# A gated feed-forward layer with quantized second product: seven-product form for the last eight slots of the first batch, weight sums moved into the second batch, down_w turned through memory

## The chip, the cores and the metric

The kernel runs on one core of one Trainium2 chip. A core has five engines with queues of their own: TensorE (PE, matmuls, with its weight loads shown as PEld), VectorE (DVE), ScalarE (ACT), GpSimd (POOL) and SyncE (SP), which here issues nearly all DMAs. Each engine works its queue in order; semaphores tie them together. The metric is device time in microseconds of one execution. The kernel before took 734.88 us, the median of three runs (734.56 to 737.32).

## The reference

`x` is 4 batches of 1024 tokens of 512 numbers, `cond` 4 x 128, `up_w` 4096 x 512, `down_w` 512 x 2048. Cut to what matters:

```
scale = cond @ norm_w.T + 1.0
h  = x * (scale[:, None, :] * rsqrt(mean(x * x) + EPS))
u  = h @ up_w.T
val, gate = split(u, 2)
h  = val * gelu(gate)                     # exact GELU
hq = round(h * 127 / max|h| per token) / scale
wq = sign-like rounding of down_w to -1, 0, 1 times its mean magnitude
y  = hq @ wq.T + x
```

All numbers are fp32. The kernel gets the precision of the first product by writing each operand as a high and a low fp16 part and adding three products of the four; the second product is exact in bf16 by fp8.

## The kernel before, in words

**Slots.** The 2048 values and 2048 gates are cut into 16 slots of 128 rows of each (`NJ` = 16). One slot of one batch is one unit of work: the product of a 128-row value block and a 128-row gate block with all 1024 tokens. Slots are numbered through the four batches: slot 16 is the first of the second batch. `H` keeps the results of 18 slots.

**Two ways to do a slot.** In the first batch, `first_batch(j)` calls `plain_half` twice. Each half is 512 tokens: `plain` does 12 matmuls for the gate (4 pieces of the 512 features, 3 high/low terms each) and 12 for the value, 48 in a slot. In the later batches `slot(g)` treats the block as a 2 x 2 block product and does it with seven products of half size in place of eight (`product`, 6 matmuls each, 42 in a slot). The price is sums: seven combinations of the token blocks (`Tokens.sums`, `XP` and `t_view`) and seven of the weight blocks (`s_sums`), again split into high and low parts.

In `slot`, TensorE does products 0, 4 and 1 of slot g, then product 3 of slot g-1, 5 of g, 2 of g-1, and 6 of g. They accumulate onto each other: ScalarE copies bank A to bank B before product 1, copies E into `v`, copies A into `t2` (that copy stands ahead of product 6, which writes the same bank), and applies the two GELUs; VectorE multiplies and adds. The hooks `early`, `x`, `y`, `z` and `mid` are places between these steps where the caller puts further work.

**Weights.** In the first batch each slot's weights are loaded (`w_load`), scaled by a power of two per row (`w_range`, `w_gain`, `w_scale`), split into high and low (`w_rows`, or TensorE's transposes for the first three slots) and turned by a transposing DMA into a tile of three that take turns (`s_tile`). The sums of the weights, needed from the second batch on, are also made in the first batch: `s_sums` on GpSimd (four 128x256 operations), `s_high` on ScalarE, `s_low` on GpSimd, and `s_spill` writes all seven to `s_dram`. Later batches fetch them with `s_load_x` and `s_load_y`; the sums of slots 3 to 15 lie there unturned and are turned on the way in.

**The rest of the first batch.** `d_load`, `d_sum`, `d_round` and `d_put` bring down_w, take its mean magnitude and round it to three values, after which a transposing DMA turns it straight into `wd`. `Tokens` prepares the second batch: norm on ScalarE and GpSimd, `scale`, `sums` on GpSimd, `high`, `low`, and a transposing DMA (`turn`). `pair_max` takes the largest magnitude of each token over slots.

**The later batches.** After a batch's last slot the largest value per token over all partitions is needed: `token_max` calls `partition_all_reduce` on GpSimd, once for each half of the tokens, in places x and z of the next batch's slot 0. `get_ready` does a dummy reduction of that kind beforehand. Then `token_scale` on VectorE, the rounding (`quant_scale`, `quant_round`, `quant_up`, `quant_down`) in slots 2 to 9 and the second product in slots 10 to 13 (`Pair`). The order of the instructions is the order in which the code is written; a small planner (`Filler`, with costs and due places) hands out the rounding work in batches 2 to 4.

Of the kernel before, what the change touches and what calls it, by code (L numbers as in the profile page):

```python
# [50 lines left out]
def glu_quant_kernel(  # L51
# [30 lines left out]
    DVE.memset(neghalf, -0.5)  # L82
    unmagic = cpool.tile([P, 1], F32, name="unmagic")
# [16 lines left out]
    s_dram = tc.dram_tile([NJ, P, 7 * 2 * HALF], F16, name="s_dram")  # L100

# [27 lines left out]
    XP = XP.rearrange("p (l k t) -> p l k t", l=2, k=NK)  # L129
    S_more = R[:, 0, 4096 : 4096 + 7 * HALF].bitcast(F16).rearrange(  # L130
        "p (c w f) -> p c w f", c=7, w=2
    )
    A21 = R[:, 0, 6144 : 6144 + 768].bitcast(F16).rearrange("p (n w f) -> p n w f", n=3, w=2)
# [12 lines left out]
    def pow2_floor(t):  # L146

        ti = t.bitcast(I32)
        DVE.tensor_scalar(ti, ti, EXPONENT, None, ALU.bitwise_and)
# [107 lines left out]
    iv = {}  # L257
# [4 lines left out]

    def wf(j):

        return H[:, 11 if j == 2 else 15 + j % 2].rearrange("p t (n f) -> p (t n) f", n=2)
# [16 lines left out]
    def w_factor(j, am, t0=0, t1=2):  # L282
        t = slice(t0, t1)
        pow2_floor(am)
        DVE.tensor_scalar(sw[:, j, t], am, 2.0**-100, 1.0 / W_UP, ALU.max, ALU.mult)
        if j not in iv:
            iv[j] = sm.tile([P, 2], F32, name=f"iv_{j}", tag="iv", bufs=3)
        DVE.reciprocal(iv[j][:, t], sw[:, j, t])
# [4 lines left out]
    def w_gain(j):  # L293
        DVE.tensor_scalar(sg0[:, j, :], sw[:, j, :], dx[:, 0:1], None, ALU.mult)
# [4 lines left out]
    LATE = 6  # L299

    def w_scale(j, ts=(1, 0), eng=None):
        eng = eng or (ACT if j >= ROWS else POOL)
        for t in ts:
            w, r = wn(j)[:, t], iv[j][:, t : t + 1]
            if eng is ACT:
                ACT.activation(w, w, AF.Copy, scale=r)
            else:
                eng.tensor_scalar(w, w, r, 1.0, ALU.mult, ALU.mult)
# [11 lines left out]
    def a_parts(j):  # L320

        s = s_tile(j)
        return s[:, 5:7], s[:, 3] if j >= ROWS else A21[:, j % 3], s[:, 4]

    def w_rows(j):
# [4 lines left out]
        ACT.copy(n[:, :, 0], f)  # L330
        DVE.tensor_tensor(n[:, :, 1], f, n[:, :, 0], ALU.subtract)
        SP.dma_start_transpose(
            s_tile(j)[:, 3:7].rearrange("p n w (k f) -> p (n w k) f", k=2), v
        )
# [19 lines left out]
    def w_evac(j):  # L354
        for n in range(2):
            ACT.copy(wf(j)[:, 2 * n : 2 * n + 2].rearrange("p n f -> p (n f)"), pw[j][n])

    def s_sums(j):
        if j >= ROWS:
            v = wn(j).rearrange("p t (n f) -> p t n f", n=2)  # L360
            a11, a12, a21, a22 = v[:, 1, 0], v[:, 1, 1], v[:, 0, 0], v[:, 0, 1]
        else:
            a11, a12, a21, a22 = (wf(j)[:, n] for n in range(4))
# [5 lines left out]
    def s_parts(j):  # L369
        s = s_tile(j)  # L370
        s4 = A21[:, j % 3 : j % 3 + 1] if j >= ROWS else s[:, 3:4]
        return (s[:, 0:3], sf[:, 0:3]), (s4, sf[:, 3:4])

    def s_high(j):
        for s, f in s_parts(j):
            ACT.copy(s[:, :, 0], f)

    def s_low(j, eng):
        for s, f in s_parts(j):
            eng.tensor_tensor(s[:, :, 1], f, s[:, :, 0], ALU.subtract)  # L380

    def s_spill(j):
        def out(c0, c1, v):
            SP.dma_start(
                out=s_dram[j, :, c0 * 2 * HALF : c1 * 2 * HALF],
                in_=v.rearrange("p c w f -> p (c w f)"),
            )

        s = s_tile(j)
        if j < ROWS:  # L390
            out(0, C_ALL, s)
            return
        out(0, 3, s[:, 0:3])
        out(4, C_ALL, s[:, 4:])
        out(3, 4, A21[:, j % 3 : j % 3 + 1])

    def s_load(g, c0, c1, turn=False):
        s, d = s_tile(g)[:, c0:c1], s_dram[g % NJ, :, c0 * 2 * HALF : c1 * 2 * HALF]
# [5 lines left out]
    def s_load_x(g):  # L404
        s_load(g, Y_TO, C_ALL)
        s_load(g, 0, Y_FROM, g % NJ >= ROWS)

    def s_load_y(g):
        if g % NJ < ROWS:
# [38 lines left out]
    def d_round(n):  # L448

        dn = d_part(n)  # L450
        ACT.activation(dn, dn, AF.Copy, scale=wsc, bias=MAGIC)
# [3 lines left out]
    def d_put(n):  # L455
# [5 lines left out]
        if y:  # L461
            SP.dma_start_transpose(wd[:, n // 4, u], tn[-1])
# [17 lines left out]
    class Tokens:  # L480
# [73 lines left out]
        def low(self, eng):  # L554
            for n, f in self.parts():
# [11 lines left out]
    def product(c, g, ps, start, stop):  # L567
# [3 lines left out]
        o = ps.rearrange("p (a t) -> p a t", t=P)  # L571
        for n, (w, l, k) in enumerate(TERMS):
            PE.matmul(  # L573
                o, s[:, w, k, :], tv[:, :, c, l, k, :],
# [24 lines left out]
    def gain(g, t):  # L599
        return sg[g // NJ][:, g % NJ, t : t + 1]  # L600
# [40 lines left out]
    def slot(  # L641
        g, x=nothing, y=nothing, z=nothing, early=nothing, mid=(nothing,) * 3, late=nothing
# [11 lines left out]
        if up:  # L654
# [4 lines left out]
            ACT.copy(pb, cur["A"])  # L659
            cur["E"] = bank("E", 2, name=f"E_{g}")  # L660
# [36 lines left out]
    def pair_max(b, i, h, pairs=1):  # L697

        v = h_slots(b * NJ + 2 * i, 2 * pairs)[:, :, h].rearrange("p j t -> p t j")
# [56 lines left out]
    def grid_of(b, i, h):  # L756
        return h_slots(b * NJ + 2 * i, 2)[:, :, h], q_view(b)[:, :, h, 2 * i : 2 * i + 2]
# [238 lines left out]
    def second_part():  # L996
# [11 lines left out]
    D_ROUND = {5: (0, 1), 6: (2,), 7: (3,), 9: (4,), 10: (5,), 11: (6,), 12: (7,)}  # L1008
    D_MEAN = 4
    TOKENS = {6: 0, 8: 1, 10: 2, 12: 3}  # L1010
    LARGEST = {
        4: (0, 0, 2), 5: (0, 1, 2), 8: (2, 0, 2), 10: (2, 1, 2), 12: (4, 0, 2), 13: (4, 1, 2),
# [548 lines left out]
```

## Time and profile before

| | |
|---|---|
| median of 3 runs | 734.88 us (734.56 to 737.32) |
| the profiled execution's own time | 733.24 us |
| its span on the core | 731.4 us |
| TensorE busy | 720.9 us, 99% |
| VectorE busy | 587.2 us, 80% |
| ScalarE busy | 396.1 us, 54% |
| GpSimd busy | 195.8 us, 27% |
| first batch, slots 0 to 15 | to 188.4 us |
| second batch begins | 188.4 us |

The profile is of one execution. A row of the timeline reads: start in us, duration, engine, line of the kernel, operation, written and read tiles, shape, how many in a row, and in square brackets how long the engine had stood idle and what ended that. "issue" names idle time in which the engine waited for nothing that the profile shows. Matmuls are pipelined, so their cost is read from the step between rows rather than from a row's duration. In the view of waits, the three numbers are the total in us, how often, and the longest.

### The profile page before, as it was taken

The numbers are of one execution on the slowest core, as the hardware profiler recorded it, in microseconds if no ns is written. First come the engines' busy times: TensorE is split into PE (matmuls) and PEld (weight loads), VectorE is DVE, ScalarE is ACT, GpSimd is POOL, SyncE is SP. The second block draws the span as 40 slices with busy tenths as digits, with TensorE's granted clock in tenths as the row PEclk, the third lists the DMA queues.
The fourth block names the chain that finished last, engine by engine and source line by source line (L and its number), as shares of the span: only waits on it lengthen the run. The fifth ranks groups of instructions, "written<-read, shape, count | busy, mean of one in ns | idle before, by whom it ended". The sixth has DMA issues, their size and how long they took to land.

```text
span 731.4 us, 10126 instructions
## 1 busy us (share of the span) xinstructions
PE 720.9 (99%) x3661; PEld 358.9 (49%) x3661; DVE 587.2 (80%) x805; ACT 396.1 (54%) x629; POOL 195.8 (27%) x207
## 2 busy tenths in 40 slices
PE   7999999999999999999999999999999999999998
PEld 3544444444444446655444445665444444445744
DVE  6977889887498899797689887787678888755897
ACT  5868875872236675444335676543433665332274
POOL 1379886666200032450010030461020000000100
PEclk9999999999999999999999999999999999999999
DMA  6759998987544554886735646756934545452253
GB/s 233 252 165 307 291 286 233 254 199 180 165 94 106 134 121 147 191 164 172 194 100 102 130 101 173 187 146 165 226 98 106 91 100 115 103 103 90 87 189 115
DMA packets 203982, 117.30 MB, mean 160 GB/s; under 512 B 165382, under 2 KB 174487, under 8 KB 203932
## 3 DMA queue, kind: packets, MB, share of 16 engines
q1 hardware_dynamic: 203642, 116.33, 62.3%
q8 instruction: 28, 0.46, 0.3%
q10 hardware_dynamic: 290, 0.33, 0.2%
q14 instruction: 22, 0.18, 0.1%
HBM read 54.22 MB, written 23.09 MB: 106 GB/s over the span
## 4 chain that ended last, share of the span: by engine, by line
PE 87%; DVE 4%; POOL 4%; DMA 2%; ACT 1%; issue 1%; SPq 0%; POOLq 0%; DVEq 0%; ACTq 0%
PE A L573 34%; PE E L573 17%; PE B L573 8%; PE po L844 8%; PE pg L588 6%; PE pv L588 6%; PE po_end L793 4%; DVE gm L707 1%; PE po L793 1%; DMA H<-in_x_dram 1%; POOL xt L529 1%; DMA SXY<-H 1%; POOL H L367 1%; PE po_B L844 0%; POOL R L380 0%
## 5 line engine op out<-in xcount | busy, mean ns | idle before, releaser
L573 PEld LDWEIGHTS <-SXY 128*128 128x128 f16 x2016 | 197.3, 98 | 232.3 <-issue 0.6
L573 PE MATMUL A<-R,SXY 128*128 128x512 f16 x1152 | 266.3, 379 | 0.0
L573 PE MATMUL E<-R,SXY 128*128 128x512 f16 x576 | 140.0, 379 | 0.1
L671 DVE SCALAR_TENSOR_TENSOR H<-A,sg,t 128x512 f32<-128x512 f32 x48 | 36.0, 750 | 73.3 <-PE A L573 73.1
L588 PEld LDWEIGHTS <-SXY 128*128 128x128 f16 x486 | 47.4, 98 | 59.0 <-issue 1.7
L765 DVE TENSOR_TENSOR H<-H,am 128x1024 f32<-128x1024 f32 x64 | 76.2, 1216 | 0.0
L723 POOL PARTITION_ALL_REDUCE am<-R x8 | 14.3, 1793 | 230.4 <-DVE R L709 230.4
L684 ACT ACTIVATE t<-t,sg 128x512 f32<-128x512 f32 x48 | 34.6, 721 | 70.3 <-DVE t L681 70.2
L707 DVE TENSOR_REDUCE gm<-H 128x512 f32<-128x1024 f32 (+1 forms) x50 | 71.6, 1433 | 0.8
L573 PE MATMUL B<-R,SXY 128*128 128x512 f16 x288 | 70.0, 379 | 0.0
L588 PE MATMUL pg<-R,SXY 128*128 128x512 f16 x252 | 57.8, 379 | 0.3 <-DMA SXY<-H 0.3
L844 PE MATMUL po<-wd,R 128*128 128x256 fp8e4 (+1 forms) x448 | 56.8, 275 | 0.0
L588 PE MATMUL pv<-R,SXY 128*128 128x512 f16 x234 | 54.4, 379 | 1.1 <-DVE H L616 1.0
L844 PEld LDWEIGHTS <-R 128*128 128x128 bf16 (+1 forms) x480 | 47.0, 98 | 12.8
L668 ACT ACTIVATE t<-B,sg 128x512 f32<-128x512 f32 x48 | 33.0, 687 | 36.5 <-PE B L573 36.5
L477 POOL TENSOR_SCALAR ssq<-ssq 128x2 f32<-128x2 f32 x12 | 3.6, 298 | 176.8 <-ACT xt L507 124.1
L651 ACT COPY t<-A 128x512 f32<-128x512 f32 x48 | 27.9, 582 | 39.5 <-PE A L573 39.2
L659 ACT COPY B<-A 128x512 f32<-128x512 f32 x48 | 27.4, 572 | 39.0 <-PE A L573 38.6
L773 ACT ACTIVATE H<-H 128x1024 f32<-128x1024 f32 x38 | 39.9, 1050 | 14.1 <-DVE H L765 14.1
L663 ACT COPY v<-E 128x512 f32<-128x512 f32 x48 | 28.1, 585 | 31.3 <-PE E L573 27.8
L690 DVE SCALAR_TENSOR_TENSOR H<-v,sg,t 128x512 f32<-128x512 f32 x48 | 36.6, 762 | 7.4 <-ACT t L684 7.4
L777 ACT ACTIVATE R<-H 128x1024 bf16<-128x1024 f32 x38 | 40.1, 1055 | 0.8
(205 smaller groups left out, 978.3 us busy)
## 6 DMA issues: line engine op xcount, KB each, us to landing
SXY<-s_dram SPq DMA_DIRECT2D x57, 256.0 KB, 3.0
s_dram<-SXY SPq DMA_DIRECT2D x18, 384.0 KB, 3.0
H<-in_L_cond_up_w_dram SPq DMA_DIRECT2D x13, 512.0 KB, 5.1
SXY<-s_dram SPq DMA_DIRECT2D x39, 128.0 KB, 3.1
xr<-in_x_dram SPq DMA_DIRECT2D x19, 256.0 KB, 3.3
out_dram<-xr SPq DMA_DIRECT2D x19, 256.0 KB, 2.6
H<-in_x_dram SPq DMA_DIRECT2D x8, 512.0 KB, 8.0
R<-in_L_cond_down_w_dram SPq DMA_DIRECT2D x8, 512.0 KB, 6.9
```

Of the source, the lines that this page charges most:

```text
L573: PE.matmul(o, s[:, w, k, :], tv[:, :, c, l, k, :], start=start and n == 0, stop=stop and n == len(TERMS) - 1, skip_group_check=True,)
L588: PE.matmul(ps, a[k // 2][:, w, k % 2, :], XP[:, l, k, h * TOK : (h + 1) * TOK], start=n == 0, stop=n == len(terms) - 1,)
L668: ACT.activation(cur["t1"], pb, AF.Gelu, scale=gain(g, 1))
L671: DVE.scalar_tensor_tensor(h_half(g - 1, 0), prev["A"], gain(g - 1, 0), prev["t1"], ALU.mult, ALU.mult)
L684: ACT.activation(prev["t2"], prev["t2"], AF.Gelu, scale=gain(g - 1, 1))
L690: DVE.scalar_tensor_tensor(h_half(g - 1, 1), prev["v"], gain(g - 1, 0), prev["t2"], ALU.mult, ALU.mult)
L707: DVE.tensor_reduce(gm[0], v, AX.X, ALU.max, apply_absolute_value=True)
L765: DVE.tensor_tensor(v, v, r.to_broadcast([P, 2, TOK]), ALU.mult)
L773: ACT.activation(v, v, AF.Copy, bias=MAGIC)
L777: ACT.activation(q, by_tile(v), AF.Copy, bias=-MAGIC)
L793: PE.matmul(po.rearrange("p (y c o) -> p y c o", c=2, o=P), q[:, a, h, j], wd8[:, :, j // n, j % n, :, y0:y1].rearrange("p c o y -> p y c o"),
L844: PE.matmul(po, w[:, j], m, start=start and j == 0, stop=stop and j == n - 1, skip_group_check=True,)
```

## The change

- **Slots 8 to 15 of the first batch** (`FAST` = 8) go through `slot` in seven-product form (`fast_slot`); slots 0 to 7 stay plain (`plain_slot`). The token sums of the first batch, which this needs, are made by the new class `First`: GpSimd adds parts of `XP`, and high and low parts go to `XT`, which lies in `wd` for that time.
- **The sums of the weights of slots 0 to 7** are not made in the first batch. `Held` loads these weights again during slots 14 to 21 (`HELD_FROM` = 14), scales them on GpSimd, adds (`sums_of`, GpSimd), casts (`high`, ScalarE), subtracts (`low`, GpSimd) and spills them unturned. `held_first` stands in `early`, `held_next` around `x`.
- **The second batch takes slot 8 first** (`of_slot`, `TURNED` = 8): 8 to 15, then 0 to 7. Slots 8 to 15 lie turned in `s_dram`; 0 to 7 are turned on the way in.
- **down_w** goes to a DRAM tile (`d_dram`) and is turned from there by `d_turn` in the second batch's slot 1. `d_round` moves from ScalarE to GpSimd.
- `pow2_floor`, `w_factor` and `w_gain` use two-tensor forms with constant tiles (`emask`, `undo_up`) in place of scalar forms. `pair_max` covers two slots each time. The places of many steps in the first batch change.

The diff, cut to its core:

```diff
+    def s_turn(j):
+        SP.dma_start_transpose(
+            s_tile(j)[:, 0:4].rearrange("p n w (k f) -> p (n w k) f", k=2), S_rows
+        )
+    class Held:
+        def __init__(self, j):
+            self.j = j
+            self.w = wpool.tile([P, 2, D], F32, name=f"hw_{j}", tag="xn", bufs=1)
+            SP.dma_start(out=self.w, in_=up_v[j])
+        def sums(self):
+            j = self.j
+            for t in range(2):
+                w = self.w[:, t]
+                POOL.tensor_scalar(w, w, iv[:, j, t : t + 1], 1.0, ALU.mult, ALU.mult)
+            self.f = wpool.tile([P, 4, HALF], F32, name=f"hf_{j}", tag="xt", bufs=1)
+            sums_of(self.w, self.f)
+        def high(self):
+            v = wpool.tile([P, C_ALL, 2, HALF], F16, name=f"hr_{self.j}", tag="nx", bufs=1)
+            self.r = v[:, 0:4]
+            ACT.copy(self.r[:, :, 0], self.f)
+        def low(self):
+            POOL.tensor_tensor(self.r[:, :, 1], self.f, self.r[:, :, 0], ALU.subtract)
+        def spill(self):
+            s_spill_rows(self.j, self.r.rearrange("p n w f -> p (n w f)"))
...
     def d_round(n):
         dn = d_part(n)
-        ACT.activation(dn, dn, AF.Copy, scale=wsc, bias=MAGIC)
+        POOL.tensor_scalar(dn, dn, wsc, MAGIC, ALU.mult, ALU.add)
...
         if y:
-            SP.dma_start_transpose(wd[:, n // 4, u], tn[-1])
+            SP.dma_start(out=d_dram[n // 2], in_=tn[-1])
+    def d_turn():
+        for n in range(1, ND, 2):
+            SP.dma_start_transpose(wd[:, n // 4, d_at(n)[1]], d_dram[n // 2])
...
-    D_ROUND = {5: (0, 1), 6: (2,), 7: (3,), 9: (4,), 10: (5,), 11: (6,), 12: (7,)}
+    D_ROUND = {4: (0, 1, 2, 3), 5: (4, 5, 6, 7)}
+    D_PUT = {4: (0, 1), 5: (2, 3), 6: (4, 5), 7: (6, 7)}
-    TOKENS = {6: 0, 8: 1, 10: 2, 12: 3}
+    TOKENS = {5: 0, 7: 1, 9: 2, 11: 3}
...
+    def held_first(g):
+        i = g - HELD_FROM
+        if 0 < i <= FAST:
+            held[i - 1].spill()
+        if 0 <= i < FAST:
+            held[i].sums()
+            if i + 1 < FAST:
+                held.append(Held(i + 1))
+    def held_next(g, then=nothing):
+        mine = 0 <= g - HELD_FROM < FAST
+        if mine:
+            held[g - HELD_FROM].high()
+        then()
+        if mine:
+            held[g - HELD_FROM].low()
...
+    def fast_slot(j, sc):
+        n = j + 2
+        t = toks.get(j)
+        odd = t is not None and j not in TOKENS
+        def early():
+            held_first(j)
+            next_tokens(j + 1)
+            if n < NJ:
+                s_sums(n)
+            if j + 5 < NJ:
+                w_load(j + 5)
+            w_next(j)
+            largest(j, 0, 1)
+        def second():
+            if t and not odd:
+                t.norm()
+            elif odd:
+                t.high()
+        def x():
+            if n < NJ:
+                s_high()
+                s_low()
+            held_next(j)
+            if j in turns:
+                turns.pop(j)()
+            if j + 1 < NJ:
+                s_spill(j + 1)
+            if t and not odd:
+                t.scale(sc)
+                t.sums()
+            elif odd:
+                t.low(0, 2, DVE)
+            else:
+                largest(j, 1, 3)
...
+            if b == 1 and j == 1:
+                d_turn()
...
-            slot(g, lambda: run("x"), lambda: run("y"), lambda: run("z"), early, mid, late)
+            x = lambda: held_next(g, lambda: run("x"))
+            slot(g, x, lambda: run("y"), lambda: run("z"), early, mid, late)
```

## The prediction

> **What bounds the kernel now.** I read the page first: busy times, clock and chain.
>
> ```profile
> span 731.4 us, 10126 instructions
> PE 720.9 (99%) x3661; PEld 358.9 (49%) x3661; DVE 587.2 (80%) x805; ACT 396.1 (54%) x629; POOL 195.8 (27%) x207
> ...
> PEclk9999999999999999999999999999999999999999
> ...
> PE 87%; DVE 4%; POOL 4%; DMA 2%; ACT 1%; issue 1%; SPq 0%; POOLq 0%; DVEq 0%; ACTq 0%
> ```
>
> TensorE is busy 99% at full clock and carries 87% of the chain. So matmuls taken away are worth their issue time, and work on another engine costs nothing until TensorE waits for it. The timeline of TensorE gives the price of a slot; here one plain slot, the two stalls late in the first batch, and a seven-product slot of the second:
>
> ```profile
> 103.35 2.75 PE L588 MATMUL pg<-R 128*128 128x512 f16 x12
> 105.94 2.75 PE L588 MATMUL pv<-R 128*128 128x512 f16 x12
> 108.53 2.75 PE L588 MATMUL pg<-R 128*128 128x512 f16 x12
> 111.12 2.75 PE L588 MATMUL pv<-R 128*128 128x512 f16 x12
> 113.71 2.75 PE L588 MATMUL pg<-R,SXY 128*128 128x512 f16 x12
> ...
> 164.39 2.75 PE L588 MATMUL pv<-R,SXY 128*128 128x512 f16 x12 [1.05 <-DVE H L616]
> 175.49 2.75 PE L588 MATMUL pv<-R 128*128 128x512 f16 x12 [0.58 <-DVE H L616]
> ...
> 210.45 1.46 PE L573 MATMUL E<-R,SXY 128*128 128x512 f16 x6
> 211.74 2.75 PE L573 MATMUL A<-R,SXY 128*128 128x512 f16 x12
> ```
>
> Twelve matmuls step 2.59 us, so one costs 0.216; a plain slot is 48 (10.36), a seven-product slot 42 (9.07).
>
> Then GpSimd, in its waits and its timeline around the end of the first batch, where the all-reduces over partitions (token_max) stand:
>
> ```profile
> POOL ready L716 <- issue: 19.0, 3, 6.7
> ...
> 176.24 0.67 POOL L380 TENSOR_TENSOR R<-H,R 128x256 f16<-128x256 f32 x1
> 182.99 0.38 POOL L716 PARTITION_ALL_REDUCE ready<-ready  x1 [6.08 <-issue]
> 191.57 1.81 POOL L723 PARTITION_ALL_REDUCE am<-R  x1 [8.20 <-DVE R L709]
> 197.82 1.78 POOL L723 PARTITION_ALL_REDUCE am<-R  x1 [4.44 <-DVE R L709]
> ```
>
> Before an all-reduce that follows ordinary arithmetic, GpSimd stands idle with nothing to wait for: 19.0 us over three times, 6.33 each. get_ready, a dummy all-reduce, takes that idle time early, when GpSimd has nothing else to do; the two real ones follow without it. The way back to arithmetic (199.6, next instruction 255.5) is hidden by a long wait.
>
> **The change, part by part.** *Taken from TensorE.* Slots 8 to 15 lose 6 matmuls each: 48 x 0.216 = **-10.4 us**; the changed program's list indeed has 48 fewer. The reduces over four slots (3.75 us) become reduces over two (1.23, plus 0.76 to merge), so the stalls at 164 and 175, with lesser ones at 158 and 172, should go: **-1.9**. Slot 8 has no predecessor and carries five products; the two missing ones run in slot 16.
>
> *Fast slots, other engines.* Per slot ScalarE has the five copies and GELUs of a seven-product slot (3.1), two weight scalings (1.4), the cast of 768 (0.8), the cast of the sums (1.0) and 1.6 or 2.1 for tokens: 8.2 of 9.07. VectorE: 2.9, w_next 2.0 to 2.7, low parts 1.0, tokens 1.5 or 3.3, reduces 2.0 each: about 70 of the 72.5 us of slots 8 to 15. GpSimd: s_sums 3.64 (0.73+1.16+0.87+0.90), s_low about 2.6 (1.89+0.74 for the same 1024 elements), token sums 3.9 and 1.0 for the root in every other slot: 11.1 and 6.2, average 8.7, plus 1.0 a slot in which s_low waits for ScalarE's cast. All fit singly, with no room. What is late first: d_round, now 8 x 1.4 = 11.1 us of GpSimd in slots 4 and 5, twice the 0.695 of 128x512. The second four run behind token sums and push s_sums(8) to about 95 us; ScalarE's cast of those sums, in slot 6's order, waits about 8 us; its next slots hold 9.0 and 8.6 of work, so the copy that opens slot 8 comes about 7 us late. Later slots add about 0.5 each. Bounds: 0, if the order's slack takes it, and 13. I take **+9**, nearer the upper end, since GpSimd has no spare time to recover. DMA could be late instead: slots 8 to 12 move 14.6 MB (loads 2.6, spills 4.6, transposes 7.4) in 42.8 us, 341 GB/s, where the busiest slot-long windows show 324; that is 45 us, 2 more, inside the same term.
>
> *Small operations.* emask and undo_up replace the scalar forms, whose mean shows the collision with GpSimd (L285 0.518, but 0.17 with GpSimd idle). VectorE does not set the end there, so nothing is booked. Weighed against the trace: "GPSIMD Engine Reference", Specifications, says GpSimd's SBUF interface collides with VectorE instructions in a two-port mode or with two SBUF inputs. By the page the new forms collide as well and save nothing; by the row they save up to 0.35 each. The sum is the same.
>
> *Early work, down_w, SP.* w_evac's six copies (3.3 us) and the sums of slots 0 to 7 leave the start; TensorE's waits for that path there were 0.3, so nothing is booked. The sums of x (eight 128x1024 on GpSimd, about 3 each) run between 26 and 56 us in place of s_sums and s_low there, and are wanted at 54 and 65. Their cover is the plain slots; gone, ScalarE would wait a few us, so 0 to 3, I take 0. down_w's four transposes move to slot 17, eight slots ahead of d_sums; SP takes 1.5 us for each (L462), behind slot loads with a slot to spare: 0. Held's spill and load wait for GpSimd at the head of SP's queue, and s_load_x of the slot after next stands behind them (slot 18's behind sums(2)); while GpSimd is late TensorE is stopped too, so 0, above that the 3 us of a landing. Later batches turn 8 of 16 slots instead of 13: nothing, as TensorE does not wait there.
>
> *Held sums, slots 14 to 21.* Each slot GpSimd does 2 x 0.695 + 3.64 = 5.03 us, ScalarE casts (1.04, high), GpSimd subtracts (2.6, low). The cast stands in ScalarE's queue ahead of the copy of A into t, and TensorE's product 6 waits for that copy (in the timelines, t starts at 6.7 and product 6 at 7.77 after a slot's first product, 203.97). So sums ending later than 7.77-0.58-1.04 = 6.15 us into a slot stop TensorE.
> - Slot 14: its weights are loaded on SP behind the transpose of slot 15's sums, whose s_low ends at 8.9 of slot 13. Issue 2.0, landing 5.1: 6.9 into slot 14; sums end at 11.9: **+5.8**. Slot 15 loads once slot 14's buffer is read, ends at 7.1: **+1.0**.
> - Slots 16, 17. The changed program's GpSimd order is: low(1), [ready], sums(2), [am 0], low(2), [am 1], sums(3), where each bracket is an all-reduce among arithmetic, so library changes there and back: six. From low(1)'s end (0.7 into slot 16): 6 x 6.33 = 38.0, ready 0.4, am 3.6, two sums 10.1, low 2.6 = 54.7. Sums(3) end at 55.4; they should at 9.07+6.15 = 15.2: **+40**.
> - The way back has no price in the trace. Below: 0, which leaves 21. Above: at the start the first such change is issued at 0.8 and GpSimd's queue goes on at 8.0, 7.2 each, which gives 43. I take 6.33, the same pair of instructions, and nearest to the upper row.
> - Slots 18 to 21: one buffer, load 5.1 + sums 5.0 against 9.07, 1.0 a slot; **+2** of 0 to 4.
>
> ```profile
> L929 POOLq MODIFY_POOL_CONFIG  x2: 11/11/11, 0.8 to 0.8; - x2
> L929 POOLq EVENT_SEMAPHORE  x1: 2575/2575/2575, 8.0 to 8.0; - x1
> ```
>
> That is the start, from the view of line 929. "GPSIMD Engine Reference", Instruction dispatch, says the first call after newly loaded code pays about 6 us that no instruction shows; the 6.33 agrees, and the page speaks against the change, since it lets no direction go free. By the page the six are 36 and the sum is 2 less.
>
> Sum: 731.4 - 10.4 - 1.9 + 9 + 5.8 + 1.0 + 40 + 2 = 776.9; 1.8 lies around the span (733.24), and the median shown is 1.6 above that run: **780 us**.
>
> **Rivals.**
> 1. *The way back is free* (code still resident): three changes fewer, 780 - 19 = 761. For it: no idle time is put down to a return. Against: the 7.2 at the start.
> 2. *No change costs anything once both libraries were used.* -38: 742. Against it: the third get_ready of the kernel still paid 6.7.
> 3. *Faster: GpSimd keeps up.* Place: slots 5 to 17. If its order runs far enough ahead of TensorE that casts are never late, only -12.3 remains, 723. It decides where all GpSimd-caused waiting falls under 12.3 us; the late load of slot 14 alone takes half of that. For it: ordinary GpSimd work is 27% of the span.
> 4. *Worse*: VectorE, slowed by GpSimd in slots 18 to 21 (8.2 to 8.4 busy of 9.07 there before), and the fast slots at their bound: 795 and more.
> That the change doesn't shorten TensorE's list is excluded by the list.
>
> **How the numbers follow.** Forecast 0.52 (own range 769 to 793), rival 1 0.17, rival 2 0.09, rival 3 0.11, rival 4 0.09, no change 0.02. The range leaves out rival 3 and half of rival 4 and reaches below rival 2: 740 to 797. Within 0.5% is about what a measurement here can tell from none. Faster 0.11, same 0.02, slower 0.87.
>
> **What would show it.** TensorE busy about 10 us less, span longer. TensorE idle before A in slots 16 and 17, some 40 us in all, released by ScalarE's copy; ScalarE waiting there for GpSimd; GpSimd idle about 6 us with "issue" before each of six changes. ScalarE waiting at about 86 to 95 us for GpSimd, TensorE waiting at slot 8. Wrong if these idle times are far shorter than 6 us, or if product 6 starts on time in slots 16 and 17.

## The result, and the profile after

The changed kernel takes 808.85 us, the median of 4 runs (807.54 to 810.39), against 734.72 us (734.16 to 737.32) for the kernel before beside it: a ratio of 1.1006, with a 95% interval of 1.0978 to 1.1033. It is slower by 74 us. The forecast was 780, the range 740 to 797: the direction held, the size did not. The profiled execution took 810.39 us with a span of 808.6.

Its page, in the lines that answer to those shown of the kernel before:

```profile
span 808.6 us, 10044 instructions
...
PE 726.2 (90%) x3613; PEld 358.3 (44%) x3613; DVE 611.5 (76%) x838; ACT 397.1 (49%) x627; POOL 241.6 (30%) x224
...
PEclk8999988998876699999999999999999999999999
...
PE 69%; POOL 8%; issue 7%; DMA 7%; ACT 4%; DVE 3%; SPq 1%; POOLq 0%; ACTq 0%; DVEq 0%
```

TensorE's list is 48 matmuls shorter, as forecast, but TensorE stands idle for 82 us, most of it in slices 6, 7 and 10 to 14 (each 20 us), where its clock dips too. GpSimd, "issue" and DMA now carry 22% of the chain.

Where the time is, the view by stretches tells. Each row is one stage of the changed kernel: the stretch, its length, busy time of PE, PEld, DVE, ACT and POOL with their instructions, then TensorE's granted clock, the busy share of the DMA engines, and GB/s. The stages are: two for the start, slots 3 to 7, slot 8, slots 9 to 13, slot 14, slot 15, slots 16 and 17, slots 18 to 21, and the rest.

```profile
0.00:23.57 23.57, 18.79 (x79) 9.80 (x80) 15.63 (x66) 13.37 (x28) 3.20 (x8) 0.86 0.65 218
23.57:57.09 33.52, 28.95 (x147) 14.38 (x145) 31.46 (x50) 16.17 (x30) 22.84 (x11) 1.00 0.48 166
57.09:109.68 52.59, 52.59 (x246) 24.02 (x247) 42.92 (x58) 38.26 (x58) 25.93 (x24) 1.00 0.77 199
109.68:129.37 19.69, 10.79 (x31) 3.75 (x30) 14.09 (x22) 10.35 (x16) 9.84 (x12) 0.65 1.02 251
129.37:184.53 55.16, 47.81 (x212) 20.96 (x211) 42.26 (x58) 35.23 (x59) 42.23 (x38) 0.97 1.00 249
184.53:204.93 20.40, 10.60 (x44) 4.36 (x43) 9.06 (x12) 4.63 (x7) 6.27 (x7) 0.79 0.73 167
204.93:214.92 9.99, 9.99 (x43) 4.36 (x42) 7.29 (x8) 3.47 (x5) 7.26 (x7) 0.91 0.69 265
214.92:274.40 59.48, 22.34 (x87) 9.19 (x86) 12.89 (x19) 8.71 (x13) 18.04 (x19) 0.69 0.33 88
274.40:317.40 43.00, 37.02 (x167) 16.30 (x166) 40.91 (x38) 22.35 (x30) 34.47 (x27) 0.99 0.52 172
317.40:808.60 491.20, 487.30 (x2570) 251.18 (x2568) 394.96 (x513) 244.53 (x386) 71.46 (x73) 1.00 0.54 137
```

Against the matmuls of each stage (0.216 us each; the start against the 50.88 us at which slot 3 began before) this gives the loss:

| stage | forecast loss | measured | how |
|---|---|---|---|
| start, to slot 3 | 0 | 6.2 | 57.09 - 50.88 |
| slot 8 | 9 for slots 8 to 13 | 13.2 | 19.69 - 30 x 0.216 |
| slots 9 to 13 | (in the 9) | 9.8 | 55.16 - 5 x 9.07 |
| slot 14 | 5.8 | 11.3 | 20.40 - 9.07 |
| slot 15 | 1.0 | 0.9 | 9.99 - 9.07 |
| slots 16, 17 | 40 | 41.3 | 59.48 - 2 x 9.07 |
| slots 18 to 21 | 2 | 6.7 | 43.00 - 4 x 9.07 |
| sum | 57.8 | 89.4 | |

89.4 less the 10.4 of matmuls and the 1.9 of old stalls is 77.1; the spans differ by 77.2. So the list of places is complete, and but for the start the places are the forecast's. The large term, slots 16 and 17, came out near its size; the fast slots, slots 8 to 13, lost 14.0 us more than forecast, and the start, slot 14 and slots 18 to 21 together 16.4 more.

The rows of TensorE's timeline at the long stalls (start, duration, line, tiles, count; in brackets the idle time before and what ended it) are in slots 8, 8, 14, 16 and 17:

```profile
116.41 2.74 PE L628 MATMUL E<-wd,R 128*128 128x512 f16 x6 [5.27 <-DMA R<-R]
122.78 2.72 PE L628 MATMUL A<-wd,R 128*128 128x512 f16 x6 [3.63 <-ACT B L715]
...
202.41 2.72 PE L628 MATMUL A<-wd,R 128*128 128x512 f16 x6 [8.44 <-ACT t L707]
...
233.46 4.74 PE L628 MATMUL A<-R,SXY 128*128 128x512 f16 x12 [10.61 <-ACT t L707]
...
271.20 4.64 PE L628 MATMUL A<-R,SXY 128*128 128x512 f16 x12 [26.53 <-ACT t L707]
```

In slots 16 and 17 it is product 6 that waits for ScalarE's copy of A, as forecast. Why that copy is late stands in GpSimd's timeline of the same stretch, here from low(1) to sums(3):

```profile
211.81 2.13 POOL L433 TENSOR_TENSOR hr<-hf,hr 128x1024 f16<-128x1024 f32 x1 [1.43 <-ACT hr L430]
219.83 0.38 POOL L773 PARTITION_ALL_REDUCE ready<-ready  x1 [5.89 <-issue]
227.63 1.36 POOL L423 TENSOR_SCALAR hw<-hw,iv 128x512 f32<-128x512 f32 x2 [7.42 <-issue]
...
239.15 2.15 POOL L780 PARTITION_ALL_REDUCE am<-R  x1 [7.30 <-DVE gm L764]
248.50 2.11 POOL L433 TENSOR_TENSOR hr<-hf,hr 128x1024 f16<-128x1024 f32 x1 [7.21 <-issue]
256.63 1.80 POOL L780 PARTITION_ALL_REDUCE am<-R  x1 [6.02 <-issue]
265.37 1.36 POOL L423 TENSOR_SCALAR hw<-hw,iv 128x512 f32<-128x512 f32 x2 [6.94 <-issue]
```

Six idle times stand before the six changes between an all-reduce and arithmetic: 5.89, 7.42, 7.30, 7.21, 6.02, 6.94. What the prediction calls a library change shows in GpSimd's queue as an instruction of its own. The views of the four lines give its count, its ns (least, median, largest), and its first and last start:

```profile
L773 POOLq MODIFY_POOL_CONFIG  x6: 7/8/11, 214.1 to 573.3; - x6
L423 POOLq MODIFY_POOL_CONFIG  x4: 83/90/98, 220.2 to 258.4; - x4
L780 POOLq MODIFY_POOL_CONFIG  x4: 1/6/12, 232.0 to 250.9; - x4
L433 POOLq MODIFY_POOL_CONFIG  x2: 98/98/98, 241.2 to 241.3; - x2
```

Two of them stand at the head of each of the six idle times (at 214.1, 220.2, 232.0, 241.2, 250.9 and 258.4; four of the first row belong to later batches), 5.7 to 7.4 us before the operation that follows. They themselves last under 0.1 us. Part of the third idle time is VectorE's: that all-reduce reads what VectorE's L766 writes only then, 7.1 us after its change began, where the other two changes to an all-reduce took 5.7. From low(1)'s end (213.94) to the end of sums(3) (269.59) pass 55.65 us; the forecast said 54.7.

### The profile page after: what moved, and what is told of

Its sections match the earlier page's. It is cut to its first block, busy times and chain, and to the rows that moved or that the text cites. A ratio compares the mean times of both kernels' runs of the same rounds, so it can differ in the third digit from the quotient of the medians.

```text
span 808.6 us, 10044 instructions
## 1 busy us (share of the span) xinstructions
PE 726.2 (90%) x3613; PEld 358.3 (44%) x3613; DVE 611.5 (76%) x838; ACT 397.1 (49%) x627; POOL 241.6 (30%) x224
## 4 chain that ended last, share of the span: by engine, by line
PE 69%; POOL 8%; issue 7%; DMA 7%; ACT 4%; DVE 3%; SPq 1%; POOLq 0%; ACTq 0%; DVEq 0%
PE A L628 29%; PE E L628 14%; PE po L903 8%; PE B L628 7%; PE po_end L852 3%; PE pg L643 3%; PE pv L643 2%; DMA SXY<-R 2%; POOL hw L423 2%; DMA R<-R 1%; DMA s_dram<-hr 1%; POOL hr L433 1%; POOL R L395 1%; ACT hr L430 1%; ACT H L322 1%
## 5 line engine op out<-in xcount | busy, mean ns | idle before, releaser
L628 PEld LDWEIGHTS <-SXY 128*128 128x128 f16 x2226 | 219.1, 98 | 312.6 <-issue 60.5
L628 PE MATMUL A<-R,SXY 128*128 128x512 f16 x1182 | 278.4, 384 | 38.9 <-ACT t L707 38.9
L628 PE MATMUL E<-R,SXY 128*128 128x512 f16 x606 | 147.3, 379 | 4.1 <-DVE t L738 4.1
L744 DVE TENSOR_TENSOR v<-A,v 128x512 f32<-128x512 f32 x56 | 38.3, 683 | 68.4 <-PE A L628 63.7
L824 DVE TENSOR_TENSOR H<-H,am 128x1024 f32<-128x1024 f32 x64 | 82.2, 1310 | 0.0
L628 PE MATMUL B<-R,SXY 128*128 128x512 f16 x318 | 77.3, 379 | 0.4 <-ACT B L715 0.3
L764 DVE TENSOR_REDUCE gm<-H 128x512 f32<-128x1024 f32 x56 | 69.0, 1232 | 1.0
L747 DVE SCALAR_TENSOR_TENSOR H<-v,sg,t 128x512 f32<-128x512 f32 x56 | 44.3, 790 | 7.5 <-ACT t L741 7.4
L766 DVE TENSOR_TENSOR R<-R,gm 128x512 f32<-128x512 f32 x56 | 43.6, 778 | 1.3
L738 DVE TENSOR_TENSOR t<-E,t 128x512 f32<-128x512 f32 x56 | 37.8, 676 | 5.6 <-PE E L628 5.5
```

Source lines behind the costliest of these rows:

```text
L628: PE.matmul(o, s[:, w, k, :], tokens(l, k), start=start and n == 0, stop=stop and n == len(TERMS) - 1, skip_group_check=True,)
L747: DVE.scalar_tensor_tensor(h_half(g - 1, 1), prev["v"], gain(g - 1, 0), prev["t2"], ALU.mult, ALU.mult)
L764: DVE.tensor_reduce(gm[0], v, AX.X, ALU.max, apply_absolute_value=True)
L766: return [largest, lambda: DVE.tensor_tensor(m, m, gm[0], ALU.max)]
L824: DVE.tensor_tensor(v, v, r.to_broadcast([P, 2, TOK]), ALU.mult)
```

## The experiments

Each kernel is one edit of the changed kernel. The time of a slot is read from TensorE's timeline, from its first matmul to the first of the next slot. Runs 1 to 9 are single executions; the times of runs 10 to 15 are medians of four.

### The library changes: taken away (1), brought together (2), and no held work (3)

```diff
-        POOL.partition_all_reduce(am[:, c], m_view(b, h), P, bass_isa.ReduceOp.max)
+        if b == 0:
+            POOL.tensor_scalar(am[:, c], m_view(b, h), 1.0, 1.0, ALU.mult, ALU.mult)
+        else: ...
...
-            elif b == 1 and j == 0:
-                get_ready()
```

> Left out: the maximum over partitions for the first batch's tokens (two all-reduces become copies on GpSimd of the same size) and the dummy all-reduce ahead of them. Everything else stays, the held sums in slots 14 to 21 too. Theory (library changes): slots 16 and 17, 59.5 us in the changed kernel, fall to 18 to 23, because only the six changes kept GpSimd; the time falls from 808.9 to 768 to 772. Rival (GpSimd is late there because of its own sums and because it waits for VectorE's reduce): the stall mostly stays, 790 or more.

Measured: 775.0 us. Slots 16 and 17 take some 26 us, 33 less than the 59.5; 5.93 us of waiting stay in slot 17. Its sums end about 3 us late, behind the copies, which wait for VectorE's reduce; then ScalarE's cast waits again, for the spill out of the one buffer:

```profile
234.47 1.04 ACT L430 CAST hr<-hf 128x1024 f16<-128x1024 f32 x1 [7.45 <-DMA s_dram<-hr]
```

SP issues that spill only at 230.33, after the four transposes of `d_turn`, which hold its queue from 223.22 for 7.01 us and which the prediction booked at 0. The theory holds for the cause; the time is 3 us above its forecast.

```diff
+    HELD_AT = (14, 15, 18, 19, 20, 21, 22, 23)
...
-        i = g - HELD_FROM
-        if 0 <= i < FAST:
+        if g in HELD_AT:
+            i = HELD_AT.index(g)
             held[i].sums()
```

> All work is done; the held sums of slots 2 to 7's weights move from slots 16 to 21 to slots 18 to 23, so that the three all-reduces follow each other and GpSimd changes its library once and back. Theory (library changes, each about 6 to 7 us, and nothing else there): 34 to 39 us less, 770 to 775; in slot 18 the way back ends after the slot's start and leaves a stall of 4 to 5 us. Rival (the sums themselves are too much for GpSimd beside the slots' own work): the stalls move with them to slots 18 to 23, 790 or more.

Measured: 776.2 us, with all work done, 1 above its forecast. The edit also moves the next batch's token work by some places. GpSimd's timeline has one change each way and the three all-reduces in a row:

```profile
217.94 0.38 POOL L773 PARTITION_ALL_REDUCE ready<-ready  x1 [5.86 <-issue]
221.40 1.81 POOL L780 PARTITION_ALL_REDUCE am<-R  x1 [3.09 <-DVE R L766]
225.95 1.78 POOL L780 PARTITION_ALL_REDUCE am<-R  x1 [2.73 <-DVE R L766]
234.84 1.36 POOL L423 TENSOR_SCALAR hw<-hw,iv 128x512 f32<-128x512 f32 x2 [7.11 <-issue]
```

Slots 16 and 17 take 9.06 each: all 41.3 us are gone. But slots 18 to 23 now take 68.9 us, 14.5 more than their matmuls; the four held slots 18 to 21 of the changed kernel cost 6.7. So the sums also cost where no change of library is near: some 2 us a slot, the 1.45 us that slot 18 of this run waits behind the way back apart. The theory holds for the changes, and half of the rival is true.

```diff
     def held_first(g):
+        return
...
-        mine = 0 <= g - HELD_FROM < FAST
+        mine = False
...
-        s, d = s_tile(g)[:, c0:c1], s_dram[of_slot(g), ...]
+        j = 8 if turn else of_slot(g)
+        s, d = s_tile(g)[:, c0:c1], s_dram[j, ...]
```

> Left out: all of the held work (loads, sums, casts, low parts and spills of slots 0 to 7's sums; the second batch reads slot 8's). The all-reduces stay. Theory (the held work is what is lost from slot 14 on): slot 14 falls by 11.3 us, slots 16 and 17 by 41.3, slots 18 to 21 by 6.7: 748 to 752, and what stays above the kernel before comes from the start and slots 8 to 13. Rival (slots 18 to 21 are slow by VectorE's own work): these four stay at 40 us or more, 753 to 758.

Measured: 748.8 us, inside the forecast. Slots 14 to 17 take 37.8 us and 18 to 21 36.26, their matmuls alone. So the held work costs 60 us, all of the loss from slot 14 on. What is left, 14.5 above the kernel before, is the first batch: its start and its fast slots lose more than the matmuls save.

One thing that slows slots 18 to 21 is that VectorE and GpSimd get in each other's way. The view of groups by form, for the slots in which the rounding begins: first the kernel before, then the changed one (count, then busy us, mean ns):

```profile
L765 DVE TENSOR_TENSOR H<-H,am 128x1024 f32<-128x1024 f32 x11 | 13.1, 1217 | 0.0
L734 DVE RECIPROCAL am<-am 128x128 f32<-128x128 f32 x8 | 7.0, 922 | 0.1
L671 DVE SCALAR_TENSOR_TENSOR H<-A,sg,t 128x512 f32<-128x512 f32 x5 | 3.8, 751 | 5.5 <-PE A L573 5.5
...
L769 DVE TENSOR_SCALAR R<-H 128x1024 bf16<-128x1024 f32 x3 | 2.1, 694 | 0.1
```

```profile
L824 DVE TENSOR_TENSOR H<-H,am 128x1024 f32<-128x1024 f32 x12 | 20.4, 1721 | 0.0
L828 DVE TENSOR_SCALAR R<-H 128x1024 bf16<-128x1024 f32 x4 | 5.4, 1342 | 0.1
L791 DVE RECIPROCAL am<-am 128x128 f32<-128x128 f32 x5 | 4.5, 924 | 0.0
...
L728 DVE SCALAR_TENSOR_TENSOR H<-A,sg,t 128x512 f32<-128x512 f32 x4 | 3.0, 746 | 1.0 <-PE A L628 1.0
```

The multiplication by `am` goes from 1217 to 1721 ns and the rounding from 694 to 1342, while GpSimd, idle there before, is busy for 34.5 of 43.0 us. Reciprocals and the operation that reads a PSUM bank stay as they were. 12 x 0.504 + 4 x 0.648 is 8.6 us more VectorE work in four slots that had 8.2 to 8.4 of 9.07 booked, and VectorE is busy for 40.91 of their 43.00 us. The Trainium skill, "GPSIMD Engine Reference", Specifications, says just this: GpSimd's SBUF interface collides with VectorE instructions in a two-port mode or with two SBUF inputs. The rows agree in which forms are hit and which are not. GpSimd's own operations lengthen too: in run 2 its addition of 128x256 at L385 takes 718 to 1707 ns in slots 18 to 23, with a median of 1440, against 713 in slots 16 and 17 of the changed kernel, where VectorE has little to do.

How TensorE comes to wait differs. In slots 18 to 21 of the changed kernel 4.1 us of its waits end with VectorE and 1.8 with ScalarE's copy of A. In slots 18 to 23 of run 2 it is 11.1 of some 11.6 us with ScalarE's copy: the cast ahead of it waits 9.7 us for GpSimd's sums and 2.6 us for the spill. No run kept the held sums and took VectorE's work away, so what share of the 2 us a slot the collision has, and what share the length of GpSimd's own chain, was not separated.

### Slot 14's load (4)

```diff
-            if j + 1 == HELD_FROM:
+            if j + 2 == HELD_FROM:
                 held.append(Held(0))
```

> The load of slot 0's held weights is issued one slot earlier, at the end of slot 12, when its buffer is free; nothing else. Theory (slot 14's stall is the late load alone): its 8.4 us and the 2.2 us of slow matmuls after it go, 797 to 800. Rival (GpSimd is behind anyway at the end of slot 13, so the sums would be late without the load): under 4 us less, 805 or more.

Measured: 802.2 us. Slot 14 takes 11.96 in place of 20.40, so the load was its cause. The whole is 2 us above its forecast: some 3 us come back as stall in slots 16 and 17 (TensorE's wait in slot 16 is 13.36 us in place of 10.61). 1.8 of them are a longer idle time before the dummy all-reduce, 7.70 us in place of 5.89; no run shows why.

### Slots 9 to 13: GpSimd, DMA, SP (5 to 9)

The changed kernel takes 55.2 us for these five slots, 45.3 of them matmuls. Five edits look for the cause:

```diff
@@ 5: no sums
-            if n < NJ:
-                s_sums(n)
...
-                s_low()
@@ 6: no spill
-            if j + 1 < NJ:
+            if j + 1 >= 13 and j + 1 < NJ:
                 s_spill(j + 1)
@@ 7: no transposes
-            if n < NJ:
+            if n == 10:
                 s_turn(n)
@@ 8: two buffers
+    S_rows2 = R[:, 1, 7168:8192].bitcast(F16)
+    def rows_at(j):
+        return S_rows2 if j in (10, 12, 14) else S_rows
@@ 9: 5 and 7 together
```

> Left out: the sums of the weights of slots 10 to 15 on GpSimd and their low parts (the cast and the transpose run on what lies in the buffer). Theory A (GpSimd's sums, and VectorE slowed by them, make the fast slots late): slots 9 to 13, 55.2 us against 45.3 of matmuls, fall to 46 to 48; slot 14 gains some 6 us as its load no longer waits behind the last low part; 790 to 795. Theory B (the DMA engines, busy the whole time in slots 8 to 12 at 240 to 280 GB/s, make them late): slots 9 to 13 stay at 54 or more, only slot 14 gains, 801 to 804.

> Left out: the spill of the weight tiles of slots 9 to 12 (0.92 MB each; the second batch reads slot 8's in their place). The DMA engines have a quarter less to move in these slots. Theory A (GpSimd): slots 9 to 13 stay at 54 to 55 us, 806 to 810. Theory B (DMA): they fall by 6 to 8 us, 800 to 803.

> Left out: the transposes of the sums of slots 11 to 15 (the products take what lies in the tile); GpSimd's sums and ScalarE's casts stay. Theory (SP's queue: its issues of transposes, 4.4 to 5.8 us each here, hold the one buffer that ScalarE casts into and push all later transfers): slots 9 to 13 fall from 55.2 to 46 to 48 us, slot 14 from 20.4 to 12 to 14 as its load is no longer behind a transpose; 793 to 797. Rival (ScalarE's and VectorE's own work for tokens sets the pace): slots 9 to 13 stay over 52, only slot 14 gains, 800 to 803.

> All work is done; the sums of slots 10, 12 and 14 are cast into a second buffer (the part of R that down_w's last piece has left), so that ScalarE's cast never waits for the transpose before it. Theory A (the single buffer makes the copy of A late): slots 9 to 13 fall by 4 to 7 us, 802 to 805. Theory B (SP and the DMA engines can't carry the transposes of a slot in 9.07 us): the wait moves from the cast to the landing and little is won, 806 to 810.

> Left out: GpSimd's sums and low parts of slots 10 to 15 and also the transposes of the sums of slots 11 to 15 (each alone won 0 and 3 us in slots 9 to 13). Theory (two limits side by side, each hidden by the other: VectorE slowed by GpSimd, and the wait for the transposes): together slots 9 to 13 fall from 55.2 to 46 to 48 us, 793 to 798. Rival (a third limit, the tokens' own chain over ScalarE, VectorE and SP): slots 9 to 13 stay at 51 to 53, 800 to 804.

| run | time, us | slots 9 to 13, us |
|---|---|---|
| changed kernel | 808.9 | 55.2 |
| 5, no sums | 809.2 | 55.4 |
| 6, no spill of 9 to 12 | 805.3 | 52.5 |
| 7, no transposes of sums | 804.3 | 52.1 |
| 8, two buffers, all work done | 808.7 | 52.5 |
| 9, no sums and no transposes | 798.2 | 47.8 |

Six executions whose edits lie elsewhere (the changed kernel and runs 1 to 4 and 14) take 55.2 to 57.1 us here, so 52.5 and less is clear of them; the whole time of a single execution moves by 3 us and more on its own (807.5 to 810.4 for the changed kernel). Run 5 refuted the first theory in the form it had: leaving out GpSimd's sums alone gains nothing. Runs 6 and 7 gave 3 us where theory said 6 and more, and run 8 missed too: 3 us in these slots, and nothing of it in the whole. But the three agree to 0.4 us, and run 8 leaves no work out: so, by these three, the 2.7 us that the transposes cost beside the sums are the wait for the one buffer. Run 9 shows the rest. Its rows for slot 8, slot 9 and slots 10 to 13:

```profile
107.75:127.68 19.93, 10.97 (x32) 3.78 (x30) 13.11 (x22) 10.52 (x15) 6.71 (x8) 0.66 1.03 253
127.68:139.20 11.52, 9.38 (x43) 4.10 (x42) 7.13 (x12) 8.04 (x16) 3.72 (x6) 1.00 1.05 272
139.20:175.46 36.26, 36.26 (x169) 16.43 (x168) 29.41 (x47) 26.89 (x44) 3.73 (x6) 1.00 0.88 238
```

From slot 10 on TensorE does not wait once; the 2.5 us left are all in slot 9. From run 7 to run 9 the sums go, and 4.3 us with them. So two limits lie side by side. One is GpSimd's sums; whether by being late themselves or by slowing VectorE was not separated. The other is the transposes out of one buffer, seen alone where the sums are left out. In run 5 ScalarE's cast into the one buffer of sums waits for the transpose out of it, and SP needs 5 us for each of these issues:

```profile
138.26 1.04 ACT L392 CAST R<-H 128x1024 f16<-128x1024 f32 x1 [2.03 <-DMA SXY<-R]
139.22 0.58 ACT L707 COPY t<-A 128x512 f32<-128x512 f32 x1
150.73 1.04 ACT L392 CAST R<-H 128x1024 f16<-128x1024 f32 x1 [4.67 <-DMA R<-R]
151.68 0.58 ACT L707 COPY t<-A 128x512 f32<-128x512 f32 x1
```

```profile
143.49 5.07 SPq L398 DMA_TRANSPOSE R<-R  x1
...
152.47 5.67 SPq L398 DMA_TRANSPOSE SXY<-R  x1
158.52 4.65 SPq L604 DMA_TRANSPOSE R<-nx  x1
```

The copy of A, which product 6 needs, stands right behind that cast. The DMA engines are full as well: from slot 8 to slot 12 of the changed kernel their share is 0.99 to 1.10, and slots 9 to 12 move 276, 279, 241 and 275 GB/s. In the plain slots 3 to 7 of the kernel before a share of 1.05 moved 302 GB/s:

```profile
50.88:103.35 52.47, 52.47 (x246) 23.99 (x247) 44.95 (x64) 44.82 (x68) 46.05 (x49) 1.00 1.05 302
```

Which of the two, SP's queue or the DMA engines behind it, sets the 5 us of an issue was not separated. That full engines stop TensorE by themselves is not shown: in run 8 they stay as full, and 2.7 us go. No run has two buffers and no sums.

### Slot 8 (10, 11)

```diff
-    D_ROUND = {4: (0, 1, 2, 3), 5: (4, 5, 6, 7)}
+    D_ROUND = {4: (0, 1, 2, 3), 6: (4, 5, 6, 7)}
...
+        if n >= FAST:
+            s_turn(n)
         if odd:
             t.turn()
         plain_half(j, 1)
-        if n >= FAST:
-            s_turn(n)
@@ 11: the same, and
-    D_PUT = {4: (0, 1), 5: (2, 3), 6: (4, 5), 7: (6, 7)}
+    D_PUT = {4: (0, 1), 5: (2, 3), 6: (4, 5), 8: (6, 7)}
```

> Four of d_round's eight operations move on GpSimd from slot 5 to slot 6, behind the sums for slot 8, and the transpose of these sums goes on SP ahead of the tokens' transpose. Theory (slot 8 is late because its sums stand behind d_round and their transpose behind the tokens' one): TensorE's waits in slot 8 (5.3 and 3.6 us, and about 4 us of matmuls at half clock after them) go, 794 to 798. Rival (ScalarE's queue is full in slots 7 to 9 and the copy of A would be late anyway): under 5 us less, 804 or more.

> The edit of slot 8 (d_round behind the sums, transpose of the sums first) and the last two of d_put's operations moved on ScalarE from the end of slot 7 into slot 8, behind the copy of A. Theory (what is left of slot 8's stall, 4.2 us, is ScalarE's queue at the end of slot 7): 3 to 4 us less than with the first edit alone (803.5), 798 to 801. Rival (ScalarE is full over slots 7 to 9 together, so it comes back in slot 9): 802 to 805.

Measured: 803.5 us (ratio to the kernel before 1.0959, interval 1.0921 to 1.0997) for the first edit, 805.2 (1.0958, 1.0929 to 1.0987) for both. The first edit takes slot 8 from 19.69 to 12.98 us: the wait of 5.27 us for the transposed sums is gone, so the rounding of down_w ahead of the sums and the tokens' transpose ahead of theirs were its cause; which of the two, the edit does not tell. The whole lies between the forecast (794 to 798) and its rival (804 and more), nearer the rival. The wait for ScalarE's copy stays, 4.15 us. The second edit halves it to 2.07, and 2.48 us turn up at the next product that waits for ScalarE: slot 8 takes 14.22, and the whole is no faster (the two runs lie within each other's spread). The rival held: ScalarE has too much to do over slots 7 to 9 together. What of it could go was not tried further.

### The start (12, 13)

```diff
@@ 12: all eight sums behind the weights of slot 5; casts at the ends of slots 3 and 4
+    POOL.tensor_scalar(later, iv[:, 5], 1.0, 1.0, ALU.mult, ALU.mult)
+    for c in (6, 4, 5, 3):
+        first.whole(c, POOL)
+    for c in (6, 4, 5, 3):
+        first.sum(c, POOL)
@@ 13: all eight behind the other batches' largest scale; casts unmoved
+    POOL.tensor_scalar(later, mx, 1.0, 1.0, ALU.mult, ALU.mult)
```

> The sums of x on GpSimd wait until the weights of slot 5 are scaled (about 55 us), out of the way of VectorE's work for the second half of x and for the other batches' scale; ScalarE's casts of them go to the ends of slots 3 and 4. Theory (GpSimd's sums slow VectorE between 28 and 55 us, 4.50 instead of 1.64 us for the two scalings, 3.24 instead of 1.75 for the products with cond): about 4 us of the 6.2 lost before slot 3 come back, 804 to 806. Rival (the early loss is the lower clock at the very start, and nothing of it is VectorE's): 807 to 810.

> All work is done; the sums of x wait on GpSimd for the largest of the other batches' scale (about 40 us) and are ordered so that the first two wanted come first; ScalarE's casts stay where they are. Theory (VectorE slowed by GpSimd between 28 and 44 us costs the 2.7 us of TensorE's wait for that largest): that wait goes, slot 3 starts 2 to 4 us earlier, 804 to 807. Rival (the slowing only moves to 42 to 62 us and costs there as much): 808 to 811.

Measured: 818.5 us (1.1157, 1.1125 to 1.1190) and 809.5 (1.1023, 1.0998 to 1.1048). Both missed as remedies, and both show the cause. In run 12 both early stalls vanish; but beside the sums VectorE's two-column operations for the next weights take 2.3 us each in place of 0.2, its subtractions for x stand in its queue behind them, and TensorE then waits 2.08 us and 4.67 us in slot 4 (the second for VectorE's sum for down_w). In run 13 the 2.69 us of waiting for `mx` vanish, and the transpose for slot 3 comes 3.81 us late in their place. So in each of the three placings VectorE's instructions beside GpSimd's sums are slowed. In the changed kernel, VectorE's timeline at 28.8 and 39.0 us shows:

```profile
28.82 4.50 DVE L988 TENSOR_SCALAR H<-H,rs 128x512 f32<-128x512 f32 x2
...
38.97 3.24 DVE L213 TENSOR_TENSOR H<-R 128x1536 f32<-128x1536 f32 x1
```

The same two rows took 1.64 and 1.75 us before. Of the 6.2 us lost here, 4.0 are the waits for `mx` and for slot 3's transpose, as far as they are new, and 2.2 go with TensorE's clock in the first 23.57 us (0.86 in this execution, 1.00 in the profile of the kernel before). In the other runs with this start, slot 3 begins at 53.65 to 56.95, so the loss here is 2.8 to 6.2 us by execution.

### The clock after a stall (14)

```diff
+        if g in WARM:                       # WARM = {14: 36, 16: 45, 17: 118}
+            pz = po_bank(f"pz_{g}")
+            w = s_tile(g)[:, 0]
+            for i in range(WARM[g]):
+                PE.matmul(pz, w[:, 0, :P], w.rearrange("p w f -> p (w f)"), start=True, stop=True)
         if up:
             product(6, g, cur["A"], False, True)
```

> TensorE is kept busy in its stalls of slots 14, 16 and 17 by 36, 45 and 118 matmuls into a bank that nothing reads, a little less than the stall's length in each. Theory (the low granted clock after a stall comes from the idle time): the 12 matmuls after the stall take 2.75 us again instead of 4.6 to 4.7, six in slot 14 1.46 instead of 2.72, and 5 to 7 us are won, 802 to 804. Rival (the clock has another cause, or the matmuls delay the product): no gain, 808 or more.

Measured: 810.1 us (1.1062, 1.1023 to 1.1101), no gain. Yet the clock did what the theory said. TensorE's rows at slots 16 and 17:

```profile
232.01 4.21 PE L628 MATMUL A<-R,SXY 128*128 128x512 f16 x12 [3.40 <-ACT t L708]
...
242.53 25.63 PE L747 MATMUL pz<-SXY 128*128 128x512 f16 x118
270.08 2.75 PE L628 MATMUL A<-R,SXY 128*128 128x512 f16 x12 [1.91 <-ACT t L708]
```

With the stall filled up to 1.91 us, the twelve matmuls take 2.75 us instead of 4.64; with 3.40 us left open they still take 4.21. But the whole did not move. What is won in slots 14 and 16 is not on the path: in slot 15 TensorE now waits 0.63 us where it did not, and product 6 of slot 17, whose time GpSimd's chain sets, comes no earlier: 156.7 us after TensorE's first stall in slot 8, against 154.8. The 1.9 us won behind slot 17's stall are on the path, and in this execution GpSimd's chain is longer by 1.5 (57.1 us in place of 55.65). The theory on the clock is right, and its price was wrong.

### Five edits together (15)

The edits of runs 2, 4, 8 and 10, and the held cast behind the copy of A (`held_next` moved from x to y).

> All work is done; five edits together: held sums in slots 14, 15 and 18 to 23, d_round and transpose order of slot 8, held load one slot earlier, second buffer of sums, and the held cast behind the copy of A on ScalarE. Sum of the single runs: 808.9 less 33 less 5 less 7, less 0 to 6 for the buffer and 0 to 5 for the cast: 752 to 764. If the edits overlap (each frees what another waits for), 765 to 775.

Measured: 755.3 us (ratio 1.0298, 1.0270 to 1.0326), all work done. That is 53.6 us less than the changed kernel and still 21 more than the kernel before. Its slots 18 to 23 take 64.4 us, 10 over their matmuls, slots 8 to 13 lose 14, the start 4 and slots 14 to 17 4. Of the waits in slots 18 to 23, 3.9 us end with VectorE and 3.6 with ScalarE's copy of B, and ScalarE's cast waits 15.4 us for GpSimd. None of the edits takes the sums from beside VectorE's work; how much of the 21 us that is was not tested, and no version here beats the kernel before.

## Why the prediction was right and wrong

**Right: the library changes.** "Six library changes" at 6.33 each and 54.7 us in all: 55.65 measured, and 40 us of loss against 41.3. That both agree so closely is partly luck: the six idle times sum to 40.8 in place of 38.0, but the work between them took 1.9 less than booked; and of the 41.3, 1.9 are matmuls at half pace behind slot 17's stall, which the forecast had not booked. The way back, for which the trace had no price, took 6.9 to 7.4, near the upper bound of 7.2 and above the value taken. Rivals 1 and 2 fall with the rows above. Runs 1 and 2 show the cause; the path from GpSimd over ScalarE's cast to product 6 was as described.

**Right in mechanism, mis-sized: slot 14.** The late load was its cause (run 4). 5.8 was forecast, 11.3 measured: the weights landed so late that the sums ended at 200.80, 16.3 us into the slot instead of 11.9. That is 4.4 of the 5.5 us missed; the rest, about 1.2, is twelve matmuls at half pace behind the stall. Slot 15's 0.9 against 1.0 is luck: TensorE does not wait there, and its 0.9 is again matmuls at half pace behind slot 14's stall; with the clock kept (run 14), a wait of 0.63 shows in their place.

**The step that failed first: the fast slots, +9 with a bound of 13; measured 23.0.** Two sentences of it were wrong. "All fit singly, with no room" looked at the engines one at a time, and its own count left none: the "72.5 us of slots 8 to 15" count slot 8 as a full one; with its five products they are 70.0, just what was booked for VectorE. Runs 5, 7 and 9 show that slots 10 to 13 run without a wait only when GpSimd's sums and the transposes both go. In slot 8, 13.2 us of the 23.0, the sums stood behind other work on GpSimd and SP (6.7 us, run 10), and ScalarE's work of three slots comes together (run 11). And the DMA estimate took 324 GB/s, the busiest window seen, for what the engines can move. At a full share slots 9 to 12 moved 276, 279, 241 and 275 GB/s. 14.6 MB at their mean of 268 would be 54.5 us instead of 45; some 17 MB were moved in the end, in 65.8 us, with the engines full all that time. That this rate set the loss is not shown; what runs 7 and 8 show is the buffer. SP's issues of transposes, booked at 1.5 us each for down_w, were not booked for the sums at all; they took up to 5.1 there, and 5.7 in run 5. What was forecast of d_round came as described, ScalarE waiting 8 us until 100.3 for the sums of slot 8; the tokens' transpose ahead of theirs on SP was missed.

**The step that failed second: VectorE beside GpSimd, booked at nothing.** For slots 18 to 21 the working took +2 for the buffer; 6.7 measured, VectorE's operations being up to 1.9 times as long (what share of the 6.7 that is stays open). For the start it took 0, arguing that the sums of x are wanted late; their own lateness cost nothing, but they slowed VectorE, which was wanted early. The rule of the Trainium skill on this was cited in the prediction and set aside with "VectorE does not set the end there". That sentence was about the small operations. The large ones beside the moved GpSimd work were never costed with it.

**Rival 4** (795 and more, chance 0.09) named VectorE's slowing in slots 18 to 21 and the fast slots at their bound; it had neither the start nor the buffer, and the bound of 13 was passed by 10. Its first half should have been no rival but a term: its condition, VectorE at 8.2 to 8.4 of 9.07 with new GpSimd work beside it, stood in the profile already.

**The gain** of 10.4 and 1.9 is in the account above, to 0.1 us.

## What to carry to other kernels

Before moving work to GpSimd, list VectorE's instructions that will stand beside it, and cost those with two SBUF inputs, or of one input and copied fast, at half as long again to twice as long. Count each alternation of an all-reduce and arithmetic on GpSimd as about 6 to 8 us in each direction, and put all such calls next to each other. Where several engines are each nearly full, taking work from one tells little: leave out two at a time.

## What was not expected of the hardware

- TensorE's matmuls ran at half pace after longer stalls (six took 2.72 us after 3.63) and at full pace after shorter ones (1.46 after 1.48). In between the length alone does not decide: in run 14 six took 2.23 after 2.01 and in run 11 2.72 after 2.07, but 1.46 after 2.29 in run 5 and after 2.74 in run 11. The Trainium skill, "TensorE: Matmul & The Clock Gate", What's actually happening, puts this down to an idle window of about 3.4 us; the rows agree in kind, but half pace also came after stalls shorter than that. In run 14 filling the gap kept the clock, and the time did not change.
- Each change between an all-reduce and ordinary arithmetic on GpSimd leaves it idle, in both directions and every time: in the changed kernel 5.89 and 6.02 us on the way out, 7.42, 7.21 and 6.94 on the way back; over all runs 5.8 to 7.7 and 6.8 to 7.9. Mostly the way back was the longer.
- A full share of the DMA engines is no fixed rate: 302 GB/s in the plain slots before, 241 to 279 in slots 9 to 12 with the transposes of the sums. But in run 7, without those transposes, these slots moved no more (243 to 281), at shares of 0.83 to 1.04.
